# A state-space scan whose inputs come from two places: every fourth state scaled on ScalarE, turned by TensorE

## The chip, the cores and the metric

The program runs on one core of one Trainium2 chip. The metric is the device time of one execution in microseconds (us), the median of the runs shown. The engines are named as the profile names them: PE is TensorE (its weight loads are PEld), DVE is VectorE, ACT is ScalarE, POOL is GpSimd and SP is the engine whose queue issues the DMAs. All data is float32.

## The reference, cut to what matters

Sixteen samples (B = 16) of 256 tokens (T) by 256 features go through a low-rank adapter, a bidirectional selective state-space layer with an MLP, a 16-head attention block with a feed-forward layer, and another such block with 16-wide heads. The change lies nearly all in the state-space layer:

```python
def _ssm(h, in_w, xproj_w, dt_bias, A_log, Dskip, out_w):
    xs, z = jnp.split(h @ in_w, 2, axis=-1)          # 512 channels each
    xs = jax.nn.silu(xs)
    proj = xs @ xproj_w
    dt = jax.nn.softplus(proj[..., :D_INNER] + dt_bias)
    Bm = proj[..., D_INNER:D_INNER + D_STATE]        # 64 states
    Cm = proj[..., D_INNER + D_STATE:]
    A = -jnp.exp(A_log)
    def step(hst, ins):
        dt_t, B_t, C_t, x_t = ins
        hst = hst * jnp.exp(dt_t[:, :, None] * A) + (dt_t * x_t)[:, :, None] * B_t[:, None, :]
        return (hst, jnp.einsum('bds,bs->bd', hst, C_t))
    ...
    y = jnp.swapaxes(ys, 0, 1) + xs * Dskip
    return y * jax.nn.silu(z) @ out_w
```

It runs once forwards and once over the reversed tokens; both results are added to the residual. For each sample and direction there are 64 states, and for each state a recurrence over 256 tokens in 512 channels.

## The kernel before, in words

A unit is one sample in one direction; there are 32, in order. The 512 channels are four chunks (IC = 4) of 128 partitions, so one state of one unit is a tile of 128 x 4 x 256, 1024 columns. The list `steps` holds all 2048 pairs of unit and state, and the main loop (L1145 on) runs over it, one state an iteration. What is issued in an iteration stands in that order in every engine's queue; the order is written out by hand, and the framework adds the semaphores. Each of the five queues is in order.

Iteration k does the following.

- `drive(k + 4)` (L913; AHEAD = 4): every fourth state loads the B rows of the next group of four (SG = 4) with a DMA that spreads them over all partitions (`load_b`, tile `bb`, two buffers), and every eighth the three C rows of a group of eight that POOL will use (`load_c`, tile `cb`). Then POOL multiplies dt*x (`dtx`) by the B row into a fresh tile `h` (L931), out of a ring of NH = 11. At state 0 ACT scales x by D into `skip`, in the same ring.
- `scan(k)` (L965): DVE runs two scans of 512 columns, two chunks each, h = decay * h + h (L974). The decays lie in PSUM, in a ring of three one-bank tiles (`decays`, ND = 3); their first column in each chunk is zero, which separates the chunks. For the reversed direction the decays are written backwards in time and h is read backwards. Then h is multiplied by the state's C row. For five of eight states DVE does that (L977) with C in PSUM (`cs`): `spread` (L955) makes it by turning one column of `cT`, repeated, with the identity on PE (L961). For the other three POOL does it (L981), with C from `cb`.
- `decay(k + 1)` (L935): ACT writes exp(dt * a) for the four chunks, an exponential each (L946), with the state's column of `a_neg` as the scale of each partition.
- `add_up(k - 2)` (L984; BEHIND = 2): PE turns the eight 128x128 blocks of h and adds them up in PSUM in `y` (two banks), token-major (L992). This frees the ring's buffer.
- One piece of the generator `pend` and three of `other` in two iterations. `pend` is `back` (the output product of the unit that ended) and `front` (projections, SiLU, softplus on ACT, with four products on POOL, for the unit after next). `other` is `rest`: the MLP, both attention blocks (`heads2`, `heads3`) and feed-forward layers of a finished sample. Their matmuls, copies, exponentials and reductions thus stand in the engines' queues between the pieces of the recurrence. SiLU and GELU need other tables on ACT than the exponentials, so each stands between two table loads.

The eight PSUM banks are three for the decays, one for `cs`, two for `y` and two for the matmuls of `front`, `back` and `rest`. After the last state, the rest of the last sample runs alone and uses the banks of the recurrence as well (`alone`).

Of the kernel before, what the change touches and what calls it, by code (L numbers as in the profile page):

```python
# [15 lines left out]
P = 128  # L16
# [7 lines left out]
EPS = 1e-5  # L24

# [29 lines left out]
def kernel(ctx: ExitStack, tc: tile.TileContext, a: dict, out: bass.AP):  # L55
# [69 lines left out]
    ND = 3  # L125
    NH = 11
# [8 lines left out]
    ps_c = ctx.enter_context(tc.tile_pool(name="ps_c", bufs=1, space=PSUM))  # L135
# [120 lines left out]
    for d in ("fwd", "bwd"):  # L256
# [3 lines left out]
        nc.vector.tensor_scalar(an, an, -1.0, None, ALU.mult)  # L260
# [6 lines left out]

    decays = [ps_y.tile([P, 2, T], F32, name=f"decay{j}") for j in range(ND)]
    for dc in decays:
        nc.vector.memset(dc[:, :, 0:1], 0.0)  # L270
# [102 lines left out]
    def front(u):  # L373
# [14 lines left out]
        xz = s2.tile([P, 2 * IC, T], F32, name="xz")  # L388
        for m in range(0, 2 * IC, 2):
# [8 lines left out]
            nc.scalar.copy(xz[:, m : m + 2], px)  # L398
        nc.scalar.activation(xz, xz, AF.Silu)
# [3 lines left out]
        for c in range(IC):  # L403
            nc.tensor.matmul(pb[:, :T], w_bc[d][:, c], xz[:, c], start=(c == 0), stop=(c == IC - 1))
# [5 lines left out]
        pt = bank1("pct")  # L410
        for t in range(NT):
            nc.tensor.transpose(pt[:, t * P : (t + 1) * P], bc[:, t * P : (t + 1) * P], ident)
        cT = s2.tile([P, NT, NS], F32, name="cT")
        nc.scalar.copy(cT, pt[:, :T].rearrange("p (t s) -> p t s", t=NT)[:, :, NS:])
        yield


        pr = s1.tile([P, IC, T], F32, name="pr")
        for m in range(0, IC, 2):
            pp = halves(bank1("pdt"))  # L420
            for j in range(2):
                for c in range(IC):
                    nc.tensor.matmul(  # L423
                        pp[:, j], w_dt[:, c, (m + j) * P : (m + j + 1) * P], xz[:, c],
                        start=(c == 0), stop=(c == IC - 1),
                    )
# [34 lines left out]
        tc.keep_in_program_order(nc.gpsimd.tensor_tensor(dtx, dt, xz[:, 0:IC], ALU.mult))  # L461
        st[u] = (xz, cT, bd, dt, dtx)
        yield

    def back(u, yg):
# [12 lines left out]
        for m in range(DC):  # L478
            xb = xs[b][:, m]
            nc.vector.scalar_tensor_tensor(  # L480
                xb, po[:, m], m_mamba[:, 4 + m, b : b + 1], xb, ALU.mult, ALU.add
# [82 lines left out]
    def heads2(q, k, v, o, rows):  # L564

        exs, exTs = {}, {}
        for i in range(16 + 3):
# [30 lines left out]
            if i % 2 and i >= 3:  # L598
                yield
                po = bank2("po")[:, :T]  # L600
                for h in (i - 3, i - 2):
                    exT = exTs.pop(h)
                    base = (h % 2) * 64
                    for kt in range(NT):
                        nc.tensor.matmul(  # L605
                            po[base : base + 64], v[:, kt, h * 64 : (h + 1) * 64], exT[:, kt],
# [57 lines left out]
    def heads3(q, k, v, oT):  # L664
# [28 lines left out]
        def values(g):  # L693
# [15 lines left out]
            for j in range(4):  # L709
                for kt in range(NT):  # L710
# [182 lines left out]
    bbs, cbs, ys, made, hs, skips = {}, {}, {}, {}, {}, {}  # L893
    cs = ps_c.tile([P, 2, T], F32, name="cs")
    steps = [(u, s) for u in range(len(units)) for s in range(NS)]
    turn = [0]

    def load_b(u, g):
        bd = st[u][2]
        bb = s3.tile([P, SG, T], F32, name="bb")  # L900
        nc.sync.dma_start(bb, bd[g * SG : (g + 1) * SG, :].partition_broadcast(P))
# [313 lines left out]
```

## Time and profile before

| | us |
|---|---|
| median of three runs (7620.87 to 7626.77) | 7624.67 |
| span of the profiled execution | 7616.3 |
| DVE busy | 6860.6 (90%) |
| POOL busy | 6843.8 (90%) |
| PE busy | 6249.2 (82%) |
| ACT busy | 5431.2 (71%) |

The span is the time of the profiled execution from its first instruction to its last; the median of the runs lies 8.4 us above it. The first decay starts at 137.5 us and the last scan at 7383.1; between them the program is the loop described above. A group's row gives the line, the engine, the operation, what is written from what and in which shapes and how often; then the busy time in total, the mean duration of one in ns, and the time that the engine stood idle just before such an instruction, with what released it. Busy times of neighbours that overlap are counted once, the means are not. The windows view gives the busy time of PE, PEld, DVE, ACT and POOL in a stretch (number of instructions in brackets), then the granted TensorE clock, the busy share of the DMA engines and GB/s. A row of waits reads: engine and line that waited, what released it, us in total, times, the longest. A row of the timeline gives the start, the duration and the number of instructions merged in it.

### The profile page before, as it was taken

To read this page: it belongs to the slowest core of one execution; us is meant where nothing else is said; L and a number is where in the kernel's file an instruction comes from. 1 tells how busy PE (TensorE), PEld (TensorE's weight loads), DVE (VectorE), ACT (ScalarE), POOL (GpSimd) and SP (SyncE) were. 2 spreads that over 40 slices of the span, in tenths; PEclk is the share of its full clock that TensorE was granted. 3 is DMA by queue.
4 is the path that set the end of the run, shared out by engine and by line. 5 is a ranking of instruction groups with operands and counts; after the bars stand their busy time and mean duration, and the time that the engine had idled before them with its cause. 6 is when DMAs were issued, how large, how long until landed. Compare 5 with 4: busy or idle time off the path is not lost.

```text
span 7616.3 us, 100847 instructions
## 1 busy us (share of the span) xinstructions
PE 6249.2 (82%) x35471; PEld 4952.4 (65%) x35471; DVE 6860.6 (90%) x6887; ACT 5431.2 (71%) x12141; POOL 6843.8 (90%) x2959
## 2 busy tenths in 40 slices
PE   7568888888888888888888888888888888888778
PEld 4456676666667666676666666666666766666655
DVE  3988999999999999999999999999999999999982
ACT  4567777777777777777777777777777777777753
POOL 3999999999999999999999999999999999999960
PEclk8679999999999999999999999999999999999999
DMA  4112232222322222232222223222232222322221
GB/s 166 54 65 92 89 102 76 87 92 88 103 85 93 80 91 95 92 103 73 88 92 91 100 86 98 78 92 93 87 106 79 94 84 89 101 91 89 73 68 49
DMA packets 331644, 675.90 MB, mean 89 GB/s; under 512 B 24724, under 2 KB 204032, under 8 KB 326784
## 3 DMA queue, kind: packets, MB, share of 16 engines
q1 hardware_dynamic: 331136, 669.44, 26.7%
q8 instruction: 280, 4.59, 0.2%
q14 instruction: 228, 1.87, 0.1%
HBM read 650.22 MB, written 10.75 MB: 87 GB/s over the span
## 4 chain that ended last, share of the span: by engine, by line
DVE 47%; POOL 15%; issue 14%; ACT 12%; PE 10%; DVEq 0%; POOLq 0%; ACTq 0%
DVE h L974 34%; POOL h L931 8%; DVE h L977 8%; ACT decay L946 5%; POOL h L981 5%; PE y L992 3%; DVE maxima L682 1%; ACT L155 1%; PE dense L500 1%; PE down L511 1%; PE bank L108 1%; PE po L605 1%; POOL uu L452 1%; POOL dt L458 1%; POOL dtx L461 1%
## 5 line engine op out<-in xcount | busy, mean ns | idle before, releaser
L974 DVE TENSOR_TENSOR_SCAN h<-decay,h 128x512 f32<-128x512 f32 x4096 | 4748.8, 1213 | 283.1 <-ACT decay L946 196.6
L931 POOL TENSOR_TENSOR h<-dtx,bb 128x1024 f32<-128x1024 f32 x2048 | 4793.5, 2367 | 129.2 <-PE y L992 128.4
L992 PE MATMUL y<-ident,h 128*128 128x128 f32 x16384 | 2385.3, 292 | 693.0 <-POOL h L981 639.1
L992 PEld LDWEIGHTS y<-ident,h 128*128 128x128 f32 x16384 | 2054.6, 151 | 1047.6 <-POOL h L981 733.1
L946 ACT ACTIVATE decay<-dt,a_neg_bwd 128x255 f32<-128x255 f32 x4096 | 1816.8, 471 | 759.9 <-DVE h L974 718.3
L946 ACT ACTIVATE decay<-dt,a_neg_fwd 128x255 f32<-128x255 f32 x4096 | 1824.6, 474 | 613.0 <-DVE h L974 571.6
L981 POOL TENSOR_TENSOR h<-h,cb 128x1024 f32<-128x1024 f32 x768 | 1813.2, 2361 | 289.8 <-DVE h L974 275.1
L977 DVE TENSOR_TENSOR h<-h,cs 128x1024 f32<-128x1024 f32 x1280 | 1533.5, 1215 | 66.2 <-PE cs L961 56.6
L961 PE MATMUL cs<-ident,cT 128*128 128x128 f32 x2560 | 521.6, 294 | 131.8 <-DVE h L977 130.3
L961 PEld LDWEIGHTS cs<-ident,cT 128*128 128x128 f32 x2560 | 331.4, 147 | 216.0 <-DVE h L977 192.0
L572 PE MATMUL sc<-k,q 64*128 64x256 f32 x960 | 293.4, 429 | 16.7 <-ACT ex L581 16.0
L393 PE MATMUL pxz<-hTm,w_in 128*128 128x256 f32 x1024 | 267.6, 388 | 15.9 <-DVE maxima L682 12.1
L679 PE MATMUL sc<-kd,qk 128*128 128x512 f32 x490 | 251.4, 614 | 33.5 <-DVE maxima L682 20.8
L700 PE MATMUL scT<-qk,kd 128*128 128x256 f32 x984 | 251.1, 386 | 28.7 <-DVE qk L691 23.2
L581 ACT ACTIVATE ex<-sc,nmax 128x256 f32<-128x256 f32 x480 | 222.7, 468 | 71.2 <-DVE nmax L577 68.5
L423 PE MATMUL pdt<-xz,w_dt 128*128 128x256 f32 x1024 | 247.3, 385 | 0.0
L572 PEld LDWEIGHTS sc<-k,q 64*128 64x128 f32 x960 | 172.6, 200 | 105.3 <-issue 34.2
L393 PEld LDWEIGHTS pxz<-hTm,w_in 128*128 128x128 f32 x1024 | 181.4, 194 | 53.1 <-DVE maxima L682 15.5
L700 PEld LDWEIGHTS scT<-qk,kd 128*128 128x128 f32 x984 | 175.5, 190 | 60.7 <-ACT pr L429 25.0
L577 DVE TENSOR_REDUCE nmax<-sc 128x2 f32<-128x512 f32 x240 | 163.9, 683 | 49.5 <-PE sc L572 48.8
L423 PEld LDWEIGHTS pdt<-xz,w_dt 128*128 128x128 f32 x1024 | 190.7, 194 | 22.2
L595 ACT COPY exT<-pt 128x512 f32<-128x512 f32 x240 | 140.0, 583 | 86.2 <-PE pt L591 84.0
(350 smaller groups left out, 7571.4 us busy)
## 6 DMA issues: line engine op xcount, KB each, us to landing
bb<-bd SPq DMA_DIRECT2D x512, 512.0 KB
cb<-bd SPq DMA_DIRECT2D x256, 384.0 KB
l2w<-in_L_cond_W_dram SPq DMA_DIRECT2D x32, 1024.0 KB
l3w<-in_L_cond_W_dram SPq DMA_DIRECT2D x32, 1024.0 KB
l1w<-in_L_cond_mlp_w_dram SPq DMA_DIRECT2D x48, 512.0 KB
w_in<-in_L_cond_fwd_in_w_dram SPq DMA_DIRECT2D x16, 1024.0 KB
w_dt<-_L_cond_fwd_xproj_w_dram SPq DMA_DIRECT2D x16, 1024.0 KB
w_in<-in_L_cond_bwd_in_w_dram SPq DMA_DIRECT2D x16, 1024.0 KB
```

Source lines behind the costliest of these rows:

```text
L393: nc.tensor.matmul(px[:, j], w_in[:, c, (m + j) * P : (m + j + 1) * P], hT[:, c], start=(c == 0), stop=(c == DC - 1),)
L423: nc.tensor.matmul(pp[:, j], w_dt[:, c, (m + j) * P : (m + j + 1) * P], xz[:, c], start=(c == 0), stop=(c == IC - 1),)
L572: nc.tensor.matmul(sc[:, t], q[base : base + 64, ch, t * P : (t + 1) * P], k[base : base + 64, ch], start=True, stop=True,)
L679: nc.tensor.matmul(sc, q[:, g, t * P : (t + 1) * P], kd[g % 2][:, 2 * i : 2 * i + 2], start=True, stop=True)
L700: nc.tensor.matmul(sc[:, kt], kd[g % 2][:, j, kt * P : (kt + 1) * P], q[:, g], start=True, stop=True)
L931: nc.gpsimd.tensor_tensor(h, st[u][4], bb.unsqueeze(1).to_broadcast([P, IC, T]), ALU.mult)
L946: nc.scalar.activation(dc[:, j, 1:T], st[u][3][:, c, when], AF.Exp, scale=a_neg[d][:, c, s : s + 1])
L961: nc.tensor.transpose(cs[:, i % 2, t * P : (t + 1) * P], st[u][1][:, t, s : s + 1].to_broadcast([P, P]), ident)
L974: nc.vector.tensor_tensor_scan(hv, dv, hv, 0.0, ALU.mult, ALU.add)
L977: nc.vector.tensor_tensor(h, h, c.unsqueeze(1).to_broadcast([P, IC, T]), ALU.mult)
L981: nc.gpsimd.tensor_tensor(h, h, c.unsqueeze(1).to_broadcast([P, IC, T]), ALU.mult)
L992: nc.tensor.matmul(ys[u][:, t, c * P : (c + 1) * P], h[:, c, t * P : (t + 1) * P], ident, start=(s == 0 and n == 0 and c == 0), stop=(s == ...
```

## The change

- One scan of 1024 columns a state in place of two of 512. The decays are written for all 256 tokens; dt's first token is set to 1e34 after it has served (a memset on POOL at the end of `front`), and `a_neg` is kept below -1e-30, so its exponential is zero and separates the chunks.
- PSUM holds two slots of two banks each in place of three decay tiles and `cs`. Even states use slot 0, odd ones slot 1. Odd states' scans write into their slot, and the C product reads it there.
- In each group of four states, the input of state 3 isn't made by POOL. ACT multiplies `xT` (dtx turned once a unit, token-major) by the state's column of `bT`, two instructions of 128x512 (`scale`), and PE turns the eight blocks into slot 1 (`put_in`). That state's decays go into an `h` tile in SBUF instead.
- All C rows come by DMA, four to a load. Even states' C products run on POOL, odd states' on DVE. `spread` is gone.
- The reversed direction is reversed once, when x and z are copied out of PSUM, and again when the output product is added.
- The ring `h` has 9 buffers in place of 11. x and z are separate tiles.
- In `heads2` and `heads3` the loops of the product with V are exchanged, so that neighbouring matmuls write different partitions of the result.

```diff
+APART, LEAST = 1e34, -1e-30
-    ND = 3
-    NH = 11
+    NH = 9
-    ps_c = ctx.enter_context(tc.tile_pool(name="ps_c", bufs=1, space=PSUM))
-        nc.vector.tensor_scalar(an, an, -1.0, None, ALU.mult)
+        nc.vector.tensor_scalar(an, an, -1.0, LEAST, ALU.mult, ALU.min)
-    decays = [ps_y.tile([P, 2, T], F32, name=f"decay{j}") for j in range(ND)]
-    for dc in decays:
-        nc.vector.memset(dc[:, :, 0:1], 0.0)
+    slots = [ps_y.tile([P, IC, T], F32, name=f"slot{j}") for j in range(2)]
...
-            nc.scalar.copy(xz[:, m : m + 2], px)
-        nc.scalar.activation(xz, xz, AF.Silu)
+            to = (xv, zv)[m // IC][:, m % IC : m % IC + 2]
+            nc.scalar.copy(to, px[:, :, ::-1] if d else px)
+        for v in (xv, zv):
+            nc.scalar.activation(v, v, AF.Silu)
...
+        bT = s2.tile([P, NT, NS], F32, name="bT")
+        nc.scalar.copy(bT, pt[:, :T].rearrange("p (t s) -> p t s", t=NT)[:, :, :NS])
...
+        tc.keep_in_program_order(nc.gpsimd.tensor_tensor(dtx, dt, xv, ALU.mult))
+        tc.keep_in_program_order(nc.gpsimd.memset(dt[:, :, 0:1], APART))
+        st[u] = (xv, zv, bd, dt, dtx, bT)
...
-                xb, po[:, m], m_mamba[:, 4 + m, b : b + 1], xb, ALU.mult, ALU.add
+                xb, po[:, m, ::-1] if d else po[:, m], m_mamba[:, 4 + m, b : b + 1], xb, ALU.mult, ALU.add
...
-                for h in (i - 3, i - 2):
-                    exT = exTs.pop(h)
-                    base = (h % 2) * 64
-                    for kt in range(NT):
+                for kt in range(NT):
+                    for h in (i - 3, i - 2):
+                        base = (h % 2) * 64
...
-            for j in range(4):
-                for kt in range(NT):
+            for kt in range(NT):
+                for j in range(4):
...
-        bb = s3.tile([P, SG, T], F32, name="bb")
-        nc.sync.dma_start(bb, bd[g * SG : (g + 1) * SG, :].partition_broadcast(P))
+        bb = s3.tile([P, SG - 1, T], F32, name="bb")
+        nc.sync.dma_start(bb, bd[g * SG : g * SG + SG - 1, :].partition_broadcast(P))
...
+    def turn(u):
+        xT = s1.tile([P, NT, DI], F32, name="xT")
+        for t in range(NT):
+            pt = bank1("pxt")
+            for c in range(IC):
+                nc.tensor.transpose(pt[:, c * P : (c + 1) * P], st[u][4][:, c, t * P : (t + 1) * P], ident)
+            nc.scalar.copy(xT[:, t], pt)
+        xTs[u] = xT
...
+        cb = s3.tile([P, SG, T], F32, name="cb")
+        nc.sync.dma_start(cb, bd[NS + g * SG : NS + (g + 1) * SG, :].partition_broadcast(P))
...
-            if s % 8 == 0:
-                load_c(u, s // 8)
+            load_c(u, s // SG)
...
+        if s % SG < SG - 1:
+            h = s3.tile([P, IC, T], F32, name="h", bufs=NH)
+            bb = bbs[u, s // SG][:, s % SG]
+            tc.keep_in_program_order(
+                nc.gpsimd.tensor_tensor(h, st[u][4], bb.unsqueeze(1).to_broadcast([P, IC, T]), ALU.mult)
+            )
+            hs[k] = h
...
+        if s % SG < SG - 1:
+            dc = slots[s % 2]
+        else:
+            dc = hs[k] = s3.tile([P, IC, T], F32, name="h", bufs=NH)
+        for c in range(IC):
+            nc.scalar.activation(dc[:, c], st[u][3][:, c], AF.Exp, scale=a_neg[d][:, c, s : s + 1])
+
+    def scale(k):
+        u, s = steps[k]
+        sx = s2.tile([P, NT, DI], F32, name="sx")
+        for t in range(NT):
+            nc.scalar.mul(sx[:, t], xTs[u][:, t], st[u][5][:, t, s : s + 1])
+        scaled[k] = sx
+
+    def put_in(k):
+        sx = scaled.pop(k)
+        for t in range(NT):
+            for c in range(IC):
+                nc.tensor.transpose(
+                    slots[1][:, c, t * P : (t + 1) * P], sx[:, t, c * P : (c + 1) * P], ident
                 )
...
     def scan(k):
         u, s = steps[k]
+        h, ps = hs[k], slots[s % 2]
+        c = cbs[u, s // SG][:, s % SG].unsqueeze(1).to_broadcast([P, IC, T])
+        if s % SG == SG - 1:
+            nc.vector.tensor_tensor_scan(flat(ps), flat(h), flat(ps), 0.0, ALU.mult, ALU.add)
         else:
+            to = ps if s % 2 else h
+            nc.vector.tensor_tensor_scan(flat(to), flat(ps), flat(h), 0.0, ALU.mult, ALU.add)
+        if s % 2:
+            nc.vector.tensor_tensor(h, ps, c, ALU.mult)
+        else:
+            tc.keep_in_program_order(nc.gpsimd.tensor_tensor(h, h, c, ALU.mult))
...
+    turn(0)
     decay(0)
-    spread(0)
-    spread(1)
...
             scan(k)
             if k + 1 < len(steps):
-                decay(k + 1)
+                if s % SG == SG - 2:
+                    put_in(k + 1)
+                else:
+                    decay(k + 1)
+                if s % SG == SG - 3:
+                    scale(k + 2)
+                    decay(k + 2)
+            if s == NS - 2 and k + 2 < len(steps):
+                turn(u + 1)
```

The order that this gives in ACT's queue, for a group of states 0 to 3: the decays of state 1, pieces, the decays of state 2, the scaling for state 3, the decays of state 3, pieces of two iterations, the decays of the next state 0, pieces.

## The prediction

> **What bounds the kernel now.** I read first the engine totals and the chain of waits on the page, then one long steady stretch of the windows view, then the costliest groups, then the waits, then the timeline of ten microseconds.
>
> ```profile
> PE 6249.2 (82%) x35471; PEld 4952.4 (65%) x35471; DVE 6860.6 (90%) x6887; ACT 5431.2 (71%) x12141; POOL 6843.8 (90%) x2959
> DVE 47%; POOL 15%; issue 14%; ACT 12%; PE 10%; DVEq 0%; POOLq 0%; ACTq 0%
> 1000.00:7000.00 6000.00, 5034.43 (x29034) 4005.77 (x29035) 5625.90 (x5630) 4462.97 (x10004) 5653.73 (x2433) 0.95 0.28 91
> ```
>
> Two engines are full together: DVE and POOL, both at 94% of the stretch (columns PE, PEld, DVE, ACT, POOL). I reckon in units, one sample in one direction, 64 states, 32 in the program. In that stretch the exponentials of L946 ran 6,766 times, 256 to a unit, so 26.43 units; a unit took 227.0 us, and in it DVE worked 212.9, POOL 213.9, ACT 168.9, PE 190.5 us. DVE lost 14.1 us a unit.
>
> ```profile
> L974 DVE TENSOR_TENSOR_SCAN h<-decay,h 128x512 f32<-128x512 f32 x4096 | 4748.8, 1213 | 283.1 <-ACT decay L946 196.6
> L931 POOL TENSOR_TENSOR h<-dtx,bb 128x1024 f32<-128x1024 f32 x2048 | 4793.5, 2367 | 129.2 <-PE y L992 128.4
> L981 POOL TENSOR_TENSOR h<-h,cb 128x1024 f32<-128x1024 f32 x768 | 1813.2, 2361 | 289.8 <-DVE h L974 275.1
> L977 DVE TENSOR_TENSOR h<-h,cs 128x1024 f32<-128x1024 f32 x1280 | 1533.5, 1215 | 66.2 <-PE cs L961 56.6
> L961 PE MATMUL cs<-ident,cT 128*128 128x128 f32 x2560 | 521.6, 294 | 131.8 <-DVE h L977 130.3
> L926 ACT ACTIVATE skip<-xz,colb 128x256 f32<-128x256 f32 x128 | 60.1, 496 | 0.0
> L946 ACT ACTIVATE decay<-dt,a_neg_fwd 128x255 f32<-128x255 f32 x4096 | 1824.6, 474 | 613.0 <-DVE h L974 571.6 <-issue 0.2
> ACT decay L946 <- DVE h L974: 1289.9, 1443, 6.2
> PE y L992 <- POOL h L981: 639.1, 255, 8.3
> POOL h L931 <- PE y L992: 128.4, 87, 5.8
> 3806.84 9.03 DVE L974 TENSOR_TENSOR_SCAN h<-decay,h 128x512 f32<-128x512 f32 x8
> 3810.32 1.68 ACT L946 ACTIVATE decay<-dt,a_neg_fwd 128x255 f32<-128x255 f32 x4 [0.64 <-DVE h L974]
> ```
>
> These show where each full engine spends its time, and that ACT mostly waits for DVE (1,290 us), DVE little for ACT (197 us). PE, too, waits for POOL's product. Eight scans in a row took 9.03 us, 1.13 each, though one lasts 1.21: neighbours overlap.
>
> **The change, per unit.**
>
> DVE. The 128 scans of 512 columns (4748.8/4096 = 1.159 us busy, 148.4 a unit) become 64 of 1024. A C product of 1024 columns takes 1.215, a product of 512 (L1173) 0.689, so one pass over a column costs 1.03 ns; a scan's 1.13 back to back is two passes over 512 (1.05) and 0.08 besides. 1024 columns then cost 2.10 + 0.08 = 2.18; I take 2.20, since not all stand back to back. Bounds: 2.10 with nothing fixed, 2.32 if joining saves nothing. A scan that writes PSUM is not in the trace; the product of h with a PSUM tile costs what that reads like, 1.215, so I take no surcharge and leave it to the upper bound. 64 x 2.20 = 140.8. C products on DVE go from 40 to 32 (1.198 busy each): 47.9 to 38.3. The rest, 16.6, stays. DVE: 212.9 to 195.7.
>
> POOL. 64 input products become 48 (none for s%4 = 3), 24 C products become 32; with four of the front, 92 operations at 213.9/92 = 2.325 become 84. With a memset of one column in each of four chunks (bounds 0.1, the smallest memset, and 0.95, 128x1024; near the small one, 0.3): 195.6 us.
>
> ACT. The exponentials stay; those of every fourth state now end in SBUF, 0.496 (the skip row, same shape and a pointer scale, SBUF to SBUF) for 0.474: 64 x 0.025 = 1.6. New are two scalings of 128x512 for each of 16 states. Not in the trace: below lies the plain copy of that shape, 0.583 (L595); above, the skip row with 256 more columns at 0.84 ns (2048 columns of L399 take 1.92 us, 1024 of L438 1.06), 0.71. I take 0.70, since pointer scale and SBUF both match: 22.4. Turning dtx and bT instead of cT: two copies and change, 1.5. ACT: 168.9 to 194.4.
>
> PE. Out go 80 turnings of C (521.6/2560 = 0.204, 16.3), in come 128 for the inputs and 8 for xT at the y row's 0.146 (2385.3/16384), 19.8: at most 194. Runs of 8 take 1.04 us in the timeline. The interleaved PV loops touch 176 us in all (L605), 5.5 a unit, of which perhaps half; PE is not the end of the chain, so I count nothing; ACT's 135 us of waiting for po is all it could give (4 a unit), and nothing if it is kept waiting by the decays anyway.
>
> DMA. B falls from 512 to 384 KB a group of four, C rises from 384 KB for eight states to 512 KB for four: 96 MB more on 676, so 0.28 busy becomes about 0.32. SP's queue now stands at each C load until the products of the group before are through, DVE's as well as POOL's; weights, kd and bd stand behind it. POOL never waited for B, which is wanted some 13 us after it is issued; C is wanted one group (12 us) and a scan after. Cover: that distance; price if gone: one landing late per group. I take zero.
>
> So four engines come out at 194 to 196 us in a unit that took 227. **Where the stalls go.** In every group of four DVE does scans S0..S3 and products after S1 and S3, 4 x 2.20 + 2 x 1.20 = 11.2 us. There were three half buffers for decays, now two whole ones. Even states use slot 0 and have a scan and a product (3.4) for their four exponentials (1.68). State 1 uses slot 1, free only when the product of state 3 ends: its exponentials must pass under S0 alone, 2.20. State 3's input is turned by PE into slot 1 under S2: 1.04 plus a hop. ACT takes its queue in order, so any other work standing in front of exponentials eats that margin: 0.5 us at the tightest, 1.5 to 2.5 over the places where pieces stand; I take 2. ACT pieces longer than that, per unit: SiLU with two table loads 4.5, GELU with two 4.5, softplus's three 3.3, half a SiLU of 3.6 and half an adapter GELU of 3.2. Over 2 us they stand out by 2.5 + 2.5 + 1.3 + 0.8 + 0.6 = 7.7, which DVE now waits and cannot regain. Behind a DVE that waits stand the next scan, POOL's C product, y on PE, the ring of h.
>
> Unit: 195.7 + 14.1 (the old loss kept) + 7.7 = 217.5, saving 9.5. ACT's own account is shorter: 194.4 and the 20.3 it waits inside its pieces ((1537 idle - 1001 for decays)/26.43) = 214.7. 32 x 9.5 = 304; from the span of 7616.3, 7312. The median of the runs is 8.4 above the span of the profiled execution, so 7321.
>
> **Rules against.** POOL's products kept between 2330 and 2478 ns whatever DVE did. The Trainium skill, "SBUF — State Buffer", section "SBUF: two separate sides", has VectorE operations with two SBUF inputs locked out against GpSimd ones. C from DMA lies in SBUF, but its partner is now in PSUM, as in each new scan. By the rule with two SBUF inputs the 32 products a unit would stand against POOL's, some 38 us, and the unit would be near 255; by the row, nothing. Another: multiplication rows say 1.2 us on DVE, 2.3 on POOL, about 1.4 on ACT for 1024 columns. "ScalarE: Activation LUTs", "Rules for kernel authors", wants multiplications on VectorE; that would put 16 x 1.2 = 19 us back on the engine that is full, and the unit would be about 237.
>
> **Rivals.**
>
> R1, everything overlaps: ACT being late, the results it waits for are ready, and the bursts pass under AHEAD = 4. For: DVE waited only 197 us for ACT at 71%. Against: four engines level. Unit 195.7 x 227.0/212.9 = 208.7, time 7616 - 32 x 18.3 + 8 = 7039. Chance 0.21.
>
> R2, slower: slot 1. The exponentials of state 1 can't start before the product of state 3 ends, and ACT's other work (168.9 - 256 x 0.4445 = 55 us a unit, 3.4 a group) lands in front of them or of S2's. If half does, 1.7 x 16 = 27 a unit: 209.8 + 27 = 237, time 7625 + 32 x 10 = 7945. It decides from 17.2 a unit, 1.1 us a group. For: one in-order queue at 89% feeding single buffers. Against: pieces mostly stand where 2 us are free. Chance 0.21.
>
> R3, the ring: NH falls from 11 to 9, so an h is reused three states after its y where it was five, and ACT's s%4 = 3 decays also draw from it. The 128 us POOL waited for y (4 a unit) tripling gives 225.5, time 7577. Chance 0.08.
>
> **How the numbers follow.** The sum holds with 0.50, in its own range 7110 to 7560 (the scan at 2.10 to 2.32 gives -6 to +8 a unit). 0.2%, 15 us, is what a measurement can tell. Faster: 0.48 + 0.21 + 0.05 = 0.74; same 0.03; slower 0.23, nearly all R2. Half of R1 lies below 7020 and half of R2 above 7760, so that range leaves out 2 in 10.
>
> **What would show it.** Right: DVE near 6,310 us busy, POOL 6,260, ACT 6,250; scans of 1024 columns at 2.2 to 2.3 us; scalings at 0.70; DVE's wait for ACT and for PE's input turnings up from 197 to some 450 us. Wrong: a scan over 2.32, POOL above 2.4 us a product, or DVE waiting over 17 us a unit more than now.

## The result, and the profile after

The changed kernel took 8,377.6 us (median of four runs, 8,373.1 to 8,385.1) where the kernel before took 7,623.4 beside it: a ratio of 1.0988, interval 1.0972 to 1.1003, slower by 754 us. I had forecast 7,321, faster.

The engine totals on the page of the changed kernel (its chain of waits covers only some 7% of the span, so it tells little here):

```profile
PE 6606.0 (79%) x37263; PEld 5275.6 (63%) x37263; DVE 6587.6 (79%) x4580; ACT 6147.6 (73%) x13323; POOL 6260.9 (75%) x2735
```

The work fell: POOL's by 583 us, to its forecast (6,261 for 6,260), DVE's by 273, half of what I had forecast. But no engine is full any more; four stand between 73 and 79%. The span is 8,383.3 us, so DVE stood idle 1,796 us, where it was 756.

The windows view of the same steady stretch as before, and the costliest groups:

```profile
1000.00:7000.00 6000.00, 4807.26 (x27487) 3851.22 (x27488) 4874.48 (x3364) 4564.15 (x9915) 4660.40 (x2026) 0.93 0.29 94
L935 POOL TENSOR_TENSOR h<-dtx,bb 128x1024 f32<-128x1024 f32 x1536 | 3610.2, 2360 | 772.6 <-PE y L989 569.6
L979 POOL TENSOR_TENSOR h<-h,cb 128x1024 f32<-128x1024 f32 x1024 | 2414.7, 2358 | 975.5 <-DVE h L975 833.1
L975 DVE TENSOR_TENSOR_SCAN h<-slot,h 128x1024 f32<-128x1024 f32 x1024 | 2336.5, 2282 | 770.7 <-ACT slot L947 731.5
L972 DVE TENSOR_TENSOR_SCAN slot<-h,slot 128x1024 f32<-128x1024 f32 x512 | 1169.3, 2284 | 271.0 <-PE slot L960 167.4
L975 DVE TENSOR_TENSOR_SCAN slot<-slot,h 128x1024 f32<-128x1024 f32 x512 | 1169.0, 2283 | 186.0 <-ACT slot L947 168.1
L977 DVE TENSOR_TENSOR h<-slot,cb 128x1024 f32<-128x1024 f32 x1024 | 1246.4, 1217 | 22.2
L953 ACT ACTIVATE sx<-xT,bT 128x512 f32<-128x512 f32 x1024 | 720.8, 714 | 226.6 <-PE slot L960 225.9
```

In the stretch 763 scalings ran, 32 to a unit, so 23.84 units; a unit took 251.6 us. In it DVE worked 204.4, POOL 195.5, ACT 191.4, PE 201.6. DVE lost 47.2 us a unit where it had lost 14.1. The last column says where: ahead of scans, for the exponentials in the slots (L947, 731.5 + 168.1) and for the turned input (L960, 167.4). Together 1,067 us; the one such wait of before, for the decays, was 197. The rise of 870 us is most of the 1,040 us by which DVE's idle time grew. The rows `h<-slot,h` are the even states, on slot 0; slot 1, with the states 1 and 3, has 168.1 and 167.4. So two thirds of the wait stand at the slot to which the prediction gave 3.4 us for exponentials of 1.68.

The waits of the changed kernel, longest first:

```profile
ACT slot L947 <- DVE h L975: 847.7, 674, 4.7
POOL h L979 <- DVE h L975: 833.1, 289, 8.6
DVE h L975 <- ACT slot L947: 731.5, 447, 41.2
POOL h L935 <- PE y L989: 569.6, 147, 8.4
```

DVE waits for ACT, ACT for DVE; POOL waits for DVE's scan and for PE's adding up. No engine leads: each waits in turn for the next. The timeline shows one such turn at slot 0:

```profile
3806.83 2.26 DVE L975 TENSOR_TENSOR_SCAN h<-slot,h 128x1024 f32<-128x1024 f32 x1
...
3809.01 1.20 DVE L977 TENSOR_TENSOR h<-slot,cb 128x1024 f32<-128x1024 f32 x1
3809.13 0.48 ACT L947 ACTIVATE slot<-dt,a_neg_fwd 128x256 f32<-128x256 f32 x1 [0.92 <-DVE h L975]
...
3809.55 0.36 ACT L609 COPY q<-po 128x256 f32<-128x256 f32 x1
3809.81 2.51 ACT L947 ACTIVATE slot<-dt,a_neg_fwd 128x256 f32<-128x256 f32 x6
...
3812.02 2.29 DVE L975 TENSOR_TENSOR_SCAN h<-slot,h 128x1024 f32<-128x1024 f32 x1 [1.21 <-ACT slot L947]
```

ACT waits 0.92 us until state 0's scan has ended and slot 0 is free; only then does it start on the exponentials of state 2, with a copy and, once the product has freed slot 1, exponentials of state 1 between them. DVE meanwhile has the product and a reduction of 0.68 us to do, and then waits 1.21 us for ACT. I counted this over the whole trace, leaving out the first wait of 41.2 us. In 607 of the 858 us in which DVE waited for exponentials in a slot, ACT was writing exponentials, of this state or for the other slot; in 204 it was at other layers' and projections' work, in 20 at scalings. And for 721 of the 858 us, the last time that ACT itself had stood idle, it had been waiting for DVE to free a slot.

### The profile page after: what moved, and what is told of

Its sections match the earlier page's. It is cut to its first block, busy times and chain, and to the rows that moved or that the text cites. A ratio compares the mean times of both kernels' runs of the same rounds, so it can differ in the third digit from the quotient of the medians.

```text
span 8383.3 us, 104260 instructions
## 1 busy us (share of the span) xinstructions
PE 6606.0 (79%) x37263; PEld 5275.6 (63%) x37263; DVE 6587.6 (79%) x4580; ACT 6147.6 (73%) x13323; POOL 6260.9 (75%) x2735
## 5 line engine op out<-in xcount | busy, mean ns | idle before, releaser
L935 POOL TENSOR_TENSOR h<-dtx,bb 128x1024 f32<-128x1024 f32 x1536 | 3610.2, 2360 | 772.6 <-PE y L989 569.6
L979 POOL TENSOR_TENSOR h<-h,cb 128x1024 f32<-128x1024 f32 x1024 | 2414.7, 2358 | 975.5 <-DVE h L975 833.1
L975 DVE TENSOR_TENSOR_SCAN h<-slot,h 128x1024 f32<-128x1024 f32 x1024 | 2336.5, 2282 | 770.7 <-ACT slot L947 731.5
L947 ACT ACTIVATE slot<-dt,a_neg_bwd 128x256 f32<-128x256 f32 x3072 | 1392.9, 469 | 629.7 <-DVE h L975 436.3
L947 ACT ACTIVATE slot<-dt,a_neg_fwd 128x256 f32<-128x256 f32 x3072 | 1381.9, 469 | 556.8 <-DVE h L975 411.4
L972 DVE TENSOR_TENSOR_SCAN slot<-h,slot 128x1024 f32<-128x1024 f32 x512 | 1169.3, 2284 | 271.0 <-PE slot L960 167.4
L975 DVE TENSOR_TENSOR_SCAN slot<-slot,h 128x1024 f32<-128x1024 f32 x512 | 1169.0, 2283 | 186.0 <-ACT slot L947 168.1
L977 DVE TENSOR_TENSOR h<-slot,cb 128x1024 f32<-128x1024 f32 x1024 | 1246.4, 1217 | 22.2
L960 PE MATMUL slot<-ident,sx 128*128 128x128 f32 x4096 | 678.0, 320 | 335.5 <-DVE h L977 323.1
L953 ACT ACTIVATE sx<-xT,bT 128x512 f32<-128x512 f32 x1024 | 720.8, 714 | 226.6 <-PE slot L960 225.9
L960 PEld LDWEIGHTS slot<-ident,sx 128*128 128x128 f32 x4096 | 566.3, 166 | 485.8 <-DVE h L977 234.0
L947 ACT ACTIVATE h<-dt,a_neg_bwd 128x256 f32<-128x256 f32 x1024 | 468.3, 495 | 9.9 <-PE y L989 9.9
L947 ACT ACTIVATE h<-dt,a_neg_fwd 128x256 f32<-128x256 f32 x1024 | 464.4, 495 | 8.1 <-PE y L989 8.1
```

Of the source, the lines that this page charges most:

```text
L935: nc.gpsimd.tensor_tensor(h, st[u][4], bb.unsqueeze(1).to_broadcast([P, IC, T]), ALU.mult)
L947: nc.scalar.activation(dc[:, c], st[u][3][:, c], AF.Exp, scale=a_neg[d][:, c, s : s + 1])
L953: nc.scalar.mul(sx[:, t], xTs[u][:, t], st[u][5][:, t, s : s + 1])
L960: nc.tensor.transpose(slots[1][:, c, t * P : (t + 1) * P], sx[:, t, c * P : (c + 1) * P], ident)
L972: nc.vector.tensor_tensor_scan(flat(ps), flat(h), flat(ps), 0.0, ALU.mult, ALU.add)
L975: nc.vector.tensor_tensor_scan(flat(to), flat(ps), flat(h), 0.0, ALU.mult, ALU.add)
```

## The experiments

"The changed kernel" below is 8,378 us, "the kernel before" 7,624. All differences are against these; ratios are to the kernel before on the same chip, with their intervals.

**The order on DVE and ACT.** The trace showed orders that the program doesn't have (S0's scan ahead of the product after S3), so I pinned the recurrence on DVE, then on ACT as well, to the order of the program: `pin` ties an instruction to the one pinned before it on its engine.

```diff
-            nc.vector.tensor_tensor(h, ps, c, ALU.mult)
+            pin(nc.vector.tensor_tensor(h, ps, c, ALU.mult))   # scans alike; second run: exponentials and scalings too
```

> The scans and C products of the recurrence are held in the order of the states on DVE (S0 S1 M1 S2 S3 M3); nothing else is changed. Theory Q (the order in DVE's queue): in the changed kernel the product of state 3 stands behind the next state 0's scan and state 2's scan before state 1's, so that DVE has nothing to do under the turning and little under the exponentials; with the order of the states it comes to 7,300 to 7,700 us. Theory S (two slots are too few in any order): within 2% of 8,378. Theory I (the input that ACT and PE make is late): within 2% of 8,378, with DVE's wait for the turning (167 us) as large or larger.

> As the run before it, and ACT's exponentials and scalings of the recurrence are held in the order of the states too. Theory Q: ACT's order is a smaller part, another 0 to 200 us less than with DVE's order alone. Theory S: within 2% of 8,378. Theory I: DVE's wait for the turning falls, because the scaling no longer stands behind exponentials of later states, and the time with it by up to 200 us.

Measured: 8,405.7 (1.1029 [1.0997, 1.1061]) and 8,478.9 (1.1126 [1.103, 1.1221]). Neither is faster. In the first, DVE now keeps the program's order in all groups, where the changed kernel had it in 178 of 512. Its waits at the slots are 941 us, for 1,067, and POOL's wait for scans rose from 833 to 1,605 (in the second to 1,778). So DVE's order is not what the change loses by: with it straightened, the wait shows at another engine.

**The size of the scan.** Two scans of 512 columns in place of one, in the same slots.

```diff
+            for i in (0, 2):
+                t2, p2, h2 = (flat(v[:, i : i + 2]) for v in (to, ps, h))
+                nc.vector.tensor_tensor_scan(t2, p2, h2, 0.0, ALU.mult, ALU.add)
...   # the scan of state 3 alike
```

> Two scans of 512 columns in place of one of 1024, all else as in the changed kernel, so that half a slot comes free 1.1 us earlier. Theory S: below 7,900 us. Theory Q: still over 8,000, unless the planner also happens to make another order. Theory I: within 2% of 8,378. The scans themselves cost DVE some 60 us more.

Measured: 8,419.1 (1.1047 [1.1015, 1.1079]), DVE busy 6,763.6. Joining the scans is worth 176 us of DVE's work and little time; smaller portions in the same two slots bring nothing back.

**The turned inputs, replaced.** POOL makes all inputs, and three of eight C products; DVE makes five, as before the change. Slots, ring of 9, long scans and C by DMA stay. A second run gives the ring its 11 buffers back.

```diff
-        if s % SG < SG - 1:
+        if True:
             h = s3.tile([P, IC, T], F32, name="h", bufs=NH)
...   # B rows for four states; every state's decays in its slot; scale, turn and put_in gone
-            to = ps if s % 2 else h
+        near = s % 8 not in (1, 4, 7)
+        to = ps if near else h
...
-        if s % 2:
+        if near:
             nc.vector.tensor_tensor(h, ps, c, ALU.mult)
```

> POOL makes the inputs of all four states again, every state's decays go to its slot, and POOL has 3 of 8 C products, DVE 5 of 8, as in the kernel before; two slots, one scan of 1024 columns, C by DMA and the ring of 9 stay. POOL and DVE then have as much to do as before (214 and 211 us a unit). Theory I: about 7,600 us. Theory S: 8,300 or more. Theory Q: between the two, by the order that the planner makes of it.

> The run without turned inputs (8,877 us) with the ring at 11 again; slots, one scan of 1024 columns and C by DMA stay. Theory R: about 7,700 to 8,000 us. If the slots, held through the scan and the C product, are what costs (theory S): over 8,600.

Measured: 8,877.4 (1.1648 [1.1615, 1.1682]) and 8,839.9 (1.1592 [1.1558, 1.1625]). DVE was busy 6,873 us and POOL 6,830 in the first, within 15 us of the kernel before; yet it took 1,250 us more. With the engines' work as it was and the turned inputs gone, the loss is larger, and the ring's two buffers bring 38 us of it back. In both runs the slots carry more than in the changed kernel: the decays of all states, where it was three in four, and the results of five states in eight, where it was four. DVE waited 871 and 861 us for the exponentials in them. POOL waited longest before its C products, 1,193 us in each run, which the waits view puts down to nothing ("issue"). In the trace all but some 120 us of this ended as a scan of DVE ended, so it isn't a wait for C's DMA.

**The ring alone.** The kernel before with NH = 9.

```diff
-    NH = 11
+    NH = 9
```

> The kernel before with a ring of 9 h in place of 11, nothing else. Theory R (the ring that was cut is what holds POOL back): most of the way to the changed kernel, 8,000 us or more. Theories B and L: 7,620 to 7,800, POOL waiting for y some 100 to 200 us longer than its 128.

Measured: 7,845.1 (1.0287 [1.0257, 1.0317]), 216 us above the kernel before beside it. The row of its waits that was 128.4 before:

```profile
POOL h L931 <- PE y L992: 336.5, 154, 7.5
```

**The recurrence alone.** Both kernels with all the layers behind the state-space layer left out.

```diff
-        hT = yield from norm3(b, m_mlp, 0)
...
```

> The kernel before, with the MLP and both attention blocks with their feed-forward layers left out (after a sample's recurrences its residual is only turned and written out); adapter, projections, the recurrence and the output product stay. It is the base for the same cut of the changed kernel. POOL has as much to do as before, 214 us a unit, DVE 14 less, so about 32 x 220 + 300 = 7,300 us.

> The changed kernel with the same parts left out. Theory B (the pieces of the other layers stand between the recurrence's instructions in the in-order queues, and with two slots and fewer h there is no depth left to pass over them): the changed kernel is then the faster of the two, 32 x 200 + 300 = 6,700 us against 7,300. Theory L (the recurrence itself runs in lockstep, whatever stands between): it stays the slower, 7,700 us or more.

Measured: 7,042.5 (0.9235 [0.9208, 0.9261]) and 7,255.5 (0.9514 [0.9486, 0.9542]). So the other layers cost the kernel before 582 us and the changed one 1,122: of the 754 us, 541 come only where the other layers run beside it, and 213 are there in the recurrence by itself. Neither theory's number came (6,700 and 7,700). DVE's waits without the other layers, in the kernel before and then in the changed one (both cut, so with other line numbers):

```profile
DVE h L840 <- PE cs L824: 294.5, 200, 3.5
DVE h L837 <- ACT decay L809: 235.7, 127, 4.2
```

```profile
DVE h L838 <- ACT slot L810: 478.8, 326, 41.5
DVE slot L835 <- PE slot L823: 394.1, 219, 8.9
DVE slot L838 <- ACT slot L810: 286.7, 242, 3.4
```

The first kernel had POOL 97% busy all the same; the second's fullest engine is POOL at 86%. Its waits at the slots come to 1,160 us, as many as with the other layers (1,067): those for exponentials fell from 900 to 766, that for the turning rose from 167 to 394. So the other layers' work on ACT is not needed for such waits. The two runs aren't quite like the others, though: the granted clock of PE was 0.77 and 0.785 in them, for 0.932 and 0.919 with the other layers. The timeline of the cut changed kernel shows one way in which it happens:

```profile
3818.75 2.39 POOL L455 TENSOR_TENSOR dt<-dt,uu 128x1024 f32<-128x1024 f32 x1
...
3821.06 2.39 POOL L798 TENSOR_TENSOR h<-dtx,bb 128x1024 f32<-128x1024 f32 x1
...
3823.38 2.38 POOL L842 TENSOR_TENSOR h<-h,cb 128x1024 f32<-128x1024 f32 x1
...
3825.81 1.57 PEld L852 LDWEIGHTS y<-ident,h 128*128 128x128 f32 x8 [3.65 <-POOL h L842]
3827.36 1.72 PEld L823 LDWEIGHTS slot<-ident,sx 128*128 128x128 f32 x8
...
3829.58 2.29 DVE L835 TENSOR_TENSOR_SCAN slot<-h,slot 128x1024 f32<-128x1024 f32 x1 [3.70 <-PE slot L823]
```

POOL had two other products in front of its C product; PE waited 3.65 us for that product, to add it up; behind it in PE's queue stood the turning of the input, though its slot had been free since 3823.7; and DVE waited 3.70 us for the turning, which itself took 1.91 us on PE at a granted clock of 0.50. One late product on POOL thus went by way of PE to DVE.

**The slot held shorter.** First, all scans write h in SBUF, so that a slot is free when its scan ends. Second, DVE's products move to the states 1 and 2, so that slot 1 waits for one product a group, not two.

```diff
-            to = ps if s % 2 else h
-            nc.vector.tensor_tensor_scan(flat(to), flat(ps), flat(h), 0.0, ALU.mult, ALU.add)
+            nc.vector.tensor_tensor_scan(flat(h), flat(ps), flat(h), 0.0, ALU.mult, ALU.add)
...   # state 3's scan writes h alike
         if s % 2:
-            nc.vector.tensor_tensor(h, ps, c, ALU.mult)
+            nc.vector.tensor_tensor(h, h, c, ALU.mult)
```

```diff
...   # state 3's scan writes h in SBUF
-            to = ps if s % 2 else h
+            to = ps if s % SG else h
...
-        if s % 2:
+        if s % SG in (1, 2):
             nc.vector.tensor_tensor(h, ps, c, ALU.mult)
```

> All scans write h in SBUF, and the C products of odd states read h there in place of the slot; nothing else. A slot then comes free when its scan ends, not a product (1.22 us) later. Slot 1's loop in a group of four was, by the rows of the changed kernel, four exponentials 1.88, scan 2.28, product 1.22, turning 1.04 to 1.9, scan 2.28, product 1.22: 9.9 to 10.8 us and six handovers, beside DVE's own 4 x 2.28 + 2 x 1.22 = 11.6; without the two products 7.5 to 8.4. Slot theory: nearly all the slack that the loop lacks is there now, so the time falls by 300 us or more, to 8,050 or less, and DVE's waits for the slots' exponentials (900 us) fall by half. Rival, lateness in the queues of PE, ACT and DVE through the other layers' pieces: within 100 us of 8,378. Third, a lock between DVE operations with two SBUF inputs and POOL: POOL's products rise above 2.36 us or DVE's above 1.22, and the time rises.

> DVE takes the C products of states 1 and 2 of a group of four in place of 1 and 3, POOL those of 0 and 3; the work of each engine is the same. Slot 1's loop loses one product (9.9 to 10.8 down to 8.7 to 9.6 us and five handovers), slot 0's gains one (8.3 to 9.5). Slot theory: the tightest loop has 1.2 us more in 14.9, so faster by 150 us or more. Rival, lateness through the other layers' pieces: within 100 us of 8,378. POOL's two products in a row (3 and the next 0) could keep it waiting longer, and the time would rise.

Measured: 9,097.0 (1.1927 [1.1893, 1.1962]) and 9,068.8 (1.189 [1.1856, 1.1925]): slower by some 700 us each, for different reasons. The groups of the first:

```profile
L976 DVE TENSOR_TENSOR h<-h,cb 128x1024 f32<-128x1024 f32 x1024 | 2152.7, 2102 | 22.1
L935 POOL TENSOR_TENSOR h<-dtx,bb 128x1024 f32<-128x1024 f32 x1536 | 4109.9, 2687 | 344.7 <-PE y L988 190.5 <-issue 149.7 <-DMA cb<-bd 3.0
L978 POOL TENSOR_TENSOR h<-h,cb 128x1024 f32<-128x1024 f32 x1024 | 2581.4, 2521 | 1411.9 <-DVE h L974 1384.9 <-PE sc L679 8.5 <-PE sc L573 2.0
```

DVE's product takes 2,102 ns with both inputs in SBUF, where it took 1,217 with one in PSUM, and POOL's products lengthen from 2,360 to 2,687 and 2,521. So this run tells of the third theory, the lock between the two engines, and not of the slot; the slot theory wasn't tried by it. In the second, POOL has two C products in a row; PE's wait for them rose from 123 to 1,172 us, and DVE's for exponentials in the slots from 900 to 1,362, of which 1,078 stand at the states 1 and 2. State 2's result now stays in slot 0 until its product, so one slot is held longer where the other is held shorter; which of this and POOL's order costs the time, the run doesn't tell.

**ACT's added work, and one more state behind.** First, the scalings left out, the unscaled tile turned in their place. Second, PE adds up the product of three states ago.

```diff
-        sx = scaled.pop(k)
+        sx = xTs[steps[k][0]]
...
-                    scale(k + 2)
```

```diff
-    AHEAD, BEHIND = 4, 2
+    AHEAD, BEHIND = 4, 3
```

> Leaves out the scaling by B on ScalarE for state 3 of each group: TensorE turns the unscaled tile, made once a unit. 1,024 instructions, 721 us of ACT, are gone; PE, DVE and POOL have the same work. Theory that ACT, as the engine that feeds the slots in one in-order queue, sets the pace: the time falls by most of 721 us, to below 7,800. Theory that the recurrence is a lockstep of all the engines, in which ACT's work is a part of the wait only where it stands in front of exponentials: a third of it, 8,100 to 8,250. Theory that PE's waiting for POOL holds up the rest: less than 80 us.

> BEHIND is 3 in place of 2: PE adds up the product of the state three iterations ago, so it waits less for POOL's C product, and the other layers' matmuls behind it in PE's queue stand less; the ring of 9 has one buffer less to spare. Theory of PE's queue: PE's wait for POOL's product (y) falls by half or more and the time by 150 us or more. Slot theory: PE's wait falls, the time stays within 100 us. Ring theory: POOL's wait for y (570 us) grows by 200 or more, and the time rises with it.

Measured: 8,268.4 (1.0841 [1.0809, 1.0872]) and 8,159.8 (1.0698 [1.0667, 1.073]). ACT's busy time falls by 567 us, the time by 109: ACT's added load is the smaller part of what the change loses. A distance of one more state brings 218, twice as much, with no work taken from any engine. Its waits:

```profile
POOL h L979 <- DVE h L975: 1194.6, 502, 8.3
DVE h L975 <- ACT slot L947: 430.9, 297, 41.3
POOL h L935 <- PE y L989: 263.9, 101, 5.6
DVE slot L975 <- ACT slot L947: 211.5, 161, 3.4
```

POOL's wait for y fell from 570 to 264, DVE's for the slots' exponentials from 900 to 642; POOL's for the scans rose by 361. But PE's wait for POOL's product, which I expected to halve, rose (123 to 482): POOL now is the one that waits for DVE. Of the forms that leave nothing out it is the fastest that I found, and it is still 7% slower than the kernel before.

**More depth still.** With BEHIND 3: a ring of 10 (room made by a single `sx`); no scalings and a ring of 11; the cut kernel with a ring of 12 (a pool of the start-up gives up one of three buffers for it). And BEHIND 3 in the kernel before.

```diff
+    NH = 10   # then 11, then 12
-        sx = s2.tile([P, NT, DI], F32, name="sx")
+        sx = s2.tile([P, NT, DI], F32, name="sx", bufs=1)   # first run only
```

> BEHIND 3 as in the run before, and a ring of 10 in place of 9; the scaled tile sx has one buffer in place of two, to make the room. Theory of depth (what was lost is the distance between neighbours in the chain POOL, DVE, POOL, PE, ring): the ring's tenth buffer brings 30 to 150 us more, 8,010 to 8,130, POOL's wait for y falls below 200. Rival, that the wait has moved to DVE's scans and POOL's products wait for them whatever the ring: within 30 us of 8,160. Against it: ACT's scalings wait for the turning of the group before (280 us already), and one buffer could make that more.

> Leaves out the scaling by B for state 3, as one run before, and has BEHIND 3 and a ring of 11, as deep as before the change. Theory of depth: the two gains (109 for the scalings, 218 for BEHIND) add up and the ring adds to them: 7,850 to 8,050; it would still be slower than the kernel before, for slots and turning remain single. Theory that depth alone is the matter: 7,650 or less. Rival, that the gains are not additive since the same waits are counted: 8,100 to 8,200.

> The changed kernel without the MLP, the attention blocks and the feed-forward layers, as one run before (7,256), with a ring of 12 and BEHIND 3. The kernel before, cut in the same way, took 7,043. Theory of depth: PE's wait for POOL's product (2,115 us) falls to less than half and the time to 7,050 or less. Rival, the slots' single buffering and DVE's order bind the recurrence by themselves: 7,150 to 7,256.

> The kernel before with BEHIND 3 in place of 2 and nothing else, its ring 11. There PE waited 639 us for POOL's product, but DVE and POOL are full at 94% of the steady stretch, so theory of depth: PE's wait falls by half, the time by no more than 60 us (7,560 to 7,630). Rival, that PE's queue holds up the other layers in both kernels alike: 7,400 to 7,500. If the ring is what is short there, POOL's wait for y grows from 128 us and the time by up to 100.

Measured: 8,206.2 (1.0768 [1.0737, 1.0799]); 8,138.7 (1.0679 [1.0648, 1.071]); 7,170.3 (0.9409 [0.9381, 0.9436]); 7,689.0 (1.0089 [1.006, 1.0119]). The tenth buffer doesn't pay for the single `sx`, whose wait for the turning rose to 356 us. Leaving out the scalings and going back to the old ring brings only 21 us over BEHIND 3 alone, so the gains of 109 and 218 don't add up, and a new wait stands there:

```profile
POOL h L979 <- DMA cb<-bd: 400.8, 281, 5.6
```

C's DMA lands too late; in the changed kernel that was 72 us. Cut and deep, the changed recurrence is still 128 us slower than the cut kernel before; POOL waits 371 us for C's DMA there too, so late C rows may be a part of those 128. And the kernel before loses 68 us by BEHIND 3, where I expected it to gain nothing or a little; POOL's wait for y rose only from 128 to 158 us there, DVE's for the attention's scores (nmax) from 49 to 141, and why that is so stays open. So depth is a part of it, some 218 us, and not the whole.

**The turned inputs, not replaced; the PV loops alone.** First, neither scaling nor turning, and nothing in their place. Second, the kernel before with only the loops of the product with V exchanged.

```diff
-                if s % SG == SG - 2:
-                    put_in(k + 1)
-                else:
+                if s % SG != SG - 2:
                     decay(k + 1)
```

```diff
-                    for kt in range(NT):
+                for kt in range(NT):
+                    for h in (i - 3, i - 2):
```

> Leaves out the turned inputs altogether: neither the scalings on ScalarE nor the turning by TensorE into slot 1, and nobody makes the input of state 3 in their place; its scan reads what state 1 left in the slot. DVE and POOL have the same work as in the changed kernel, ACT 721 us less, PE some 680 less; slots, ring of 9, scans of 1024 and C by DMA stay. If the turned inputs are what the change loses by: 7,650 or less. If the two whole-state slots, with the ring and the pieces of the other layers in the same queues, are: 8,100 to 8,270, little below the run without the scalings.

> The kernel before with the loops of the product with V interleaved in both attention blocks, and nothing else. In the changed kernel these matmuls were busy 155 us for 176 in one block and 89 for 89 in the other, so PE does 21 us less; PE isn't the end of the chain: 7,605 to 7,635, no difference that can be told. If the pieces of the other layers in PE's queue hold up DVE already here: 7,560 to 7,600.

Measured: 8,238.0 (1.0806 [1.079, 1.0822]) and 7,621.3 (0.9997 [0.9987, 1.0006]). The turned inputs, scaling and turning together, are 140 of the 754 us, as far as leaving them out tells: no engine made state 3's input in their place. The PV loops make no difference. DVE's waits in the first of these:

```profile
DVE slot L975 <- ACT slot L947: 452.8, 226, 8.1
DVE nmax L578 <- PE sc L573: 293.5, 75, 10.5
DVE h L975 <- ACT slot L947: 236.7, 142, 41.2
```

Even with ACT and PE relieved, DVE waits 690 us for exponentials, where the kernel before let it wait 197. No wait for C's DMA shows in this run, so late C rows are not what it still loses.

## Why the prediction was wrong

**The terms of work held, but for DVE's.** POOL was forecast at 195.6 us a unit and came to 195.5; ACT at 194.4 and 191.4; a scaling at 0.70 us and 0.714, the exponentials into SBUF at 0.496 and 0.495. A scan that writes PSUM costs 2,283 or 2,284 ns, one that writes SBUF 2,282: no surcharge, as assumed. But a scan of 1024 columns was taken at 2.20 and took 2.28, near the upper bound of 2.32. Back to back the price was right: where one long scan followed another without a gap (696 times), it started 0.083 us before the other's end, as the short ones did by 0.09. But two in three of the long scans stand behind a wait or another operation, so their busy time, overlaps counted once, came to 144.2 us a unit for 140.8. With 0.6 for the products, and 4.7 in the rest, DVE is at 204.4 for 195.7; the other operations' own work hardly changed (25.8 us for 26.0), and it is their overlaps with scans and products that went. PE came to 201.6 for at most 194: a turned input took 678.0/512 = 1.32 us, for 1.04 to 1.17, some 2.4 of the 7.6 above it (16 x 0.15); the rest I can't lay to a row. The 1.32 is a mean of two prices, by the granted clock. The windows view of the turnings alone, at two places:

```profile
279.50:282.50 3.00, 1.94 (x8) 1.57 (x8) 0.50 0.05 15
604.40:605.90 1.50, 1.06 (x8) 0.86 (x8) 1.00 0.00 0
```

Of the 512 turnings, 332 took less than 1.15 us, at a granted clock of 1.00 on the mean, and 121 more than 1.8 us, at 0.51. That is a small part of the loss: in the steady stretch the granted clock was 0.93 for 0.95, and DVE's waits for the turning are 167 us in all.

**The step that failed** is "Unit: 195.7 + 14.1 (the old loss kept) + 7.7", and in it the wait at the slots. DVE's loss was 47.2, not 21.8, and its waits at the slots rose from 197 to 1,067 us, 27.2 us a unit, where the sum had 7.7 for them. Most of this stands where the prediction saw room, "Even states use slot 0 and have a scan and a product (3.4) for their four exponentials (1.68)": 731.5 us there, and 335.5 at slot 1. One of the prediction's own signs of being wrong came with it: DVE waits 33.1 us a unit more than before, over 17. Of the 34.1 us a unit by which the forecast missed, 8.7 are work and 25.4 are this; 34.1 x 32 = 1,091, and 7,321 + 1,091 = 8,412, close to the 8,378 measured. I had kept the old loss although the change takes away what, as I now think, had kept it small: three half buffers of decays became two whole ones that also hold inputs and results, the ring lost two buffers, and DVE and POOL, each full before, so that lateness elsewhere was covered, became two of four equal engines. That this is why is argued; no run takes the pieces apart. The margin of 2 us that ACT's pieces were measured against isn't there: in the cut kernel, where ACT works 1,220 us less, most of it such pieces, the waits at the slots were 1,160 us.

**R2** named the right kind of wait, ACT's exponentials for the slots, and forecast slower. That its price of 27 us a unit agrees with the rise of 870/32 = 27.2 is luck: it was reckoned for state 1's exponentials and state 2's, and 430 us of the wait (41 of them before the first scan of all) stand at state 0. Its reason holds for a part: ACT was at other work in 204 of the 858 us, and at scalings in 20. But without the other layers the waits were as long, and without the scalings, 22.5 us of ACT's work a unit, the time fell by 109/32 = 3.4. **R3**'s price was right too: the smaller ring costs the kernel before 216 us, where R3 has 256; but I set it beside the sum with a chance of 0.08, where POOL's wait for y (570 us, for 128) shows it at work together with the slots. And a larger ring brings only 38 us back in the kernel with long scans and no turned inputs: what is missing at one place is waited for at another. R1, that lateness passes under the bursts, falls with the same rows. R2 and R3 weren't alternatives: the waits of both are in the changed kernel's rows (slots 1,067 us, POOL for y 570). That they would add up is not shown, and the runs with BEHIND 3 speak against it.

**Terms put at zero.** The PV loops: zero, shown. C by DMA: 72 us of POOL's waiting in the changed kernel, but 401 and 371 in two of the runs with BEHIND 3 and a larger ring; the cover of "one group and a scan" is not enough there. SP's queue did stand at the C loads for DVE's products, 2,595 us in all; what that delays behind it, no run isolates.

**The lock.** The prediction weighed the rule of the Trainium skill, "SBUF — State Buffer", "SBUF: two separate sides", that a DVE operation with two SBUF inputs and a GpSimd operation that reads SBUF exclude each other, and let the row decide: one input in PSUM, no lock. The row was right for this kernel (POOL stays at 2,360 ns), and the run that gave DVE's products two SBUF inputs agrees with the rule: they went from 1,217 to 2,102 ns and the kernel lost 719 us. Odd states' results go through PSUM and hold a slot longer, but it is the better of the two. The other rule, "ScalarE: Activation LUTs", "Rules for kernel authors", wants multiplications on VectorE; no run put these there, and leaving them out on ScalarE took 109 us of the 754 away.

**A sentence to correct.** I wrote of the kernel before that its instructions stand in every queue in the order of an iteration. They don't: the eight scans in a row in the timeline that I showed, over four states, have no product between them. The framework put DVE's into another order, which the trace alone shows; POOL's products are marked to keep the program's. My margins for the slots were reckoned on an order that the kernel doesn't have; but with that order on DVE the kernel took 8,406 us, so the sum would have failed with the right order too.

**What stays open.** Taken one at a time, the distance between POOL's product and PE (BEHIND) is worth 218 us and the turned inputs about 140. The larger rest goes with what all slow versions share, two whole-state slots and C by DMA. C's rows came late in some of them, but in the run without turned inputs, at 8,238 us, not at all. For the slots speak DVE's waits, their tracing back to slots freed late, and the run with the work of before and a ring of 11 (8,840). That is argued and not shown: the run that would show it, the kernel before with two whole-state slots and nothing else, was not made. Nor is it known through which queue the other layers cost the changed kernel 541 us more than the kernel before. The attempts to free the slots sooner ran into the lock and into POOL's order. Three slots weren't tried, as PSUM has no bank left, nor an order written out for PE, where the timeline shows the turning behind an adding up that it doesn't need.

## What to carry to other kernels

Here DVE lost 14 us of a unit of 227 while it and POOL were full, and 47 of 252 as one of four level engines: where a change levels the engines and takes buffers away, the loss of before can't be carried into the sum. Before pricing such a change, follow each buffer round its loop (written, read, freed, written), in the order that the trace shows, and ask what the reader has to do while it is filled again: in the turn shown at slot 0 that was a product and a reduction, 1.8 us together, and the exponentials were done 2.8 us after the slot came free. And rivals that name different waits can all happen at once: ask whether they do before giving them chances that exclude each other.

## What was not expected of the hardware

A product of 128x1024 float32 on DVE with both inputs in SBUF took 2,102 ns beside POOL's products and 1,217 with one input in PSUM; POOL's own went from 2,360 to between 2,521 and 2,687 ns. A scan of 1024 columns took 2.28 us whether it wrote PSUM or SBUF and whichever of its two inputs lay in PSUM. Back to back, each started 0.083 us before the end of the one before. Joining two scans of 512 columns saved 176/2048 = 0.09 us of DVE's busy time. Eight turnings of 128x128 on PE took 1.06 us at a granted clock of 1.00 and 1.94 at 0.50.
